# Attention stage of a four-layer kernel: one unit per row with all four heads, and a rewritten order of work

## The chip, the cores and the metric

The kernel runs on one core of one Trainium2 chip. The metric is the device time of one execution in microseconds (us), lower is better. The engines are named as in the profile: PE is TensorE (PEld its weight loads), DVE is VectorE, ACT is ScalarE, POOL is GpSimd, SP is SyncE, which here only issues DMAs. PEclk is the share of the TensorE clock that the chip granted.

## The reference, cut to what matters

A 256 x 256 grid of positions with 128 channels goes through four layers. Each layer adds its result to its input. The change concerns the first one, an attention with four heads of 32 channels along every row of the grid:

```python
z = layernorm(groupnorm(x))                      # 256 x 256 x 128
q, k, v = heads(z @ Wq), heads(z @ Wk), heads(z @ Wv)   # 4 heads of 32
g = sigmoid(heads(z @ Wg)); bias = z @ Wb        # bias: 256 x 256 x 4
scores = einsum('bijhd,bikhd->bijkh', q, k) / sqrt(32) + bias[:, None]
a = softmax(scores, axis=-2)                     # over k, within one row i
o = einsum('bijkh,bikhd->bijhd', a, v)
x = x + (g * o).reshape(b, n, n, 128) @ Wout
```

So every row i of 256 positions is its own attention problem: four 256 x 256 score matrices, one for each head.

## The kernel before

The stages follow one another: statistics of x, `row_norm` (layer norm and the bias projection, written to memory as `zs` and `bs`), `attention`, then layers 1 to 3. All data are 32-bit floats. A matmul of such data is recorded as two MATMULs (two passes), each with its weight load; a transpose is one.

`attention` holds channels on the partitions and positions along the free axis. It works in 32 blocks (NB) of 2048 positions, that is 8 rows. For a block, `load_block` issues two DMAs of 1 MB on SP (z and x), and `project` makes q, k, v and g in sixteen pieces of 512 positions, each through the PSUM tile `mm`; q and g are taken out by ACT (L287, L289), k and v by DVE (L285, L281).

A unit u is one row and a pair of heads (hp), so a block has 16 units (UB) and the stage 512. For one unit:

- `scores`: for two tiles of queries (jt) and two heads (h), q times k with 32 channels on the partitions (L297). Each head sits on its own 32 partitions, so the two heads use two row tiles of the PE array and write into two PSUM banks. Then DVE adds the bias and takes the row's minimum of the negative in four instructions (L308), which also write the result to `e`.
- `exps`: four exponentials on ACT with their sums (L323), a reciprocal on DVE (L331), the scaling of `e` on POOL (L332).
- `transposes`: eight 128 x 128 transposes into `tp0` and `tp1` (L341), taken out by ACT (L344) and DVE (L346) as `at0` and `at1`.
- `product`: v times the transposed weights (L355), 32 output columns for each head, so the two heads use two column tiles of the array, accumulated over kt into `op`.

`gate` (L369, DVE) multiplies a finished row of `op` by the gate. `out` (L382 to L386), for every second row, multiplies by Wout into `mm`, adds x on DVE, takes the statistics on DVE, and with each block's last one stores x1.

`manual_schedule()` keeps every engine's instructions in the order in which the code issues them. The loop over u issues: the gate of a row finished in the turn before, scores of u + 2, exponentials of u + 1, transposes of u, projections of the next block (in turns 5 to 15 of a block, two of them in turns 5 to 9), product of u - 1, and `out` where it is due. [...] two buffers of two banks for the scores, `tp0`, `tp1`, `op`, `mm`.

The four-tile helper `four` in `row_norm` (L167) matters as well: it issues four matmuls of 512 columns with 32 output columns each, into four 32-partition strips of one bank.

Of the kernel before, what the change touches and what calls it, by code (L numbers as in the profile page):

```python
# [10 lines left out]
F32 = mybir.dt.float32  # L11
AF = mybir.ActivationFunctionType
ALU = mybir.AluOpType
# [4 lines left out]
P = 128  # L18
S = 256
# [216 lines left out]
def attention(c, x, x1, zs, bs, w, stats):  # L236
# [3 lines left out]
    tc, nc = c.tc, c.nc  # L240
    BL, NH = 2048, 4
    NB = NPOS // BL
    UB = 16
    N = UB * NB
    with ExitStack() as a:
        one = a.enter_context(tc.tile_pool(name="l0b_one", bufs=1))
        io = a.enter_context(tc.tile_pool(name="l0b_io", bufs=2))
        wk = a.enter_context(tc.tile_pool(name="l0b_wk", bufs=2))
        ps2 = a.enter_context(tc.tile_pool(name="l0b_p2", bufs=2, space=PSUM))
        ps1 = a.enter_context(tc.tile_pool(name="l0b_p1", bufs=1, space=PSUM))  # L250
        bias = one.tile([P, NH, 2, S], F32, name="l0b_bias")

        wo = one.tile([P, P], F32, name="l0b_wo")
        nc.vector.tensor_scalar(wo, w["o"], 0.5, None, ALU.mult)
        for jt in range(2):
            nc.sync.dma_start(
                bias[:, :, jt, :], bs[:, bass.ts(jt, P), :].rearrange("h p k -> p h k")
            )
        blocks, es, tops, dens, ats, ops, gates = ({} for _ in range(7))

        def load_block(b):
            k = blocks[b] = {}
            for n, src in (("z", zs), ("x", x)):
                k[n] = io.tile([P, BL], F32, name=f"l0b_{n}")
                nc.sync.dma_start(k[n], src[:, bass.ts(b, BL)])
            for n in "qkg":
                k[n] = wk.tile([P, BL], F32, name=f"l0b_{n}")
            k["v"] = wk.tile([P, 16, P], F32, name="l0b_v")

        def project(b, i):  # L270
            k = blocks[b]
            j, n = i // 4, "kqvg"[i % 4]
            cs = bass.ts(j, CH)
            bank = ("mm", "tp0", "tp1")[i % 3] if b == 0 else "mm"
            mm = ps1.tile([P, CH], F32, name=f"l0b_{bank}")
            if n == "v":
                for m in range(4):
                    nc.tensor.matmul(
                        mm[:, bass.ts(m, P)], k["z"][:, bass.ts(4 * j + m, P)], w["v"], start=True, stop=True
                    )  # L280
                nc.vector.tensor_copy(k["v"][:, 4 * j : 4 * j + 4].rearrange("p m o -> p (m o)"), mm)  # L281
                return
            nc.tensor.matmul(mm, w[n], k["z"][:, cs], start=True, stop=True)
            if n == "k":
                nc.vector.tensor_copy(k["k"][:, cs], mm)  # L285
            elif n == "q":
                nc.scalar.activation(k["q"][:, cs], mm, AF.Copy, scale=float(1.0 / np.sqrt(32)))  # L287
            else:
                nc.scalar.activation(k["g"][:, cs], mm, AF.Tanh, scale=0.5)  # L289

        def scores(u):
            k, r, hp = blocks[u // UB], u % UB // 2, u % 2
            sc = ps2.tile([P, 2, 2, S], F32, name="l0b_sc")
            for jt in range(2):
                for h in range(2):
                    hs = slice(32 * (2 * hp + h), 32 * (2 * hp + h) + 32)
                    nc.tensor.matmul(  # L297
                        sc[:, h, jt],
                        k["q"][hs, bass.ds(r * S + jt * P, P)],
                        k["k"][hs, bass.ts(r, S)],  # L300
                        start=True,
                        stop=True,
                    )

            e = es[u] = wk.tile([P, 4, S], F32, name="l0b_e", bufs=4)
            top = tops[u] = wk.tile([P, 4], F32, name="l0b_top")
            for i in range(4):
                nc.vector.tensor_tensor_reduce(  # L308
                    e[:, i],
                    sc[:, i // 2, i % 2],  # L310
                    bias[:, 2 * hp + i // 2, i % 2],
                    -1.0,
                    3.0e38,
                    ALU.add,
                    ALU.min,
                    accum_out=top[:, i : i + 1],
                )

        def exps(u):
            e, top = es[u], tops.pop(u)  # L320
            den = wk.tile([P, 4], F32, name="l0b_den")
            for i in range(4):
                nc.scalar.activation(  # L323
                    e[:, i],
                    e[:, i],
                    AF.Exp,
                    scale=-1.0,
                    bias=top[:, i : i + 1],
                    accum_out=den[:, i : i + 1],
                )  # L330
            nc.vector.reciprocal(den, den)  # L331
            nc.gpsimd.tensor_tensor(e, e, den[:, :, None].to_broadcast([P, 4, S]), ALU.mult)  # L332

        def transposes(u):
            e = es.pop(u)
            for kt in range(2):
                tp = ps1.tile([P, CH], F32, name=f"l0b_tp{kt}")
                tp = tp.rearrange("p (h j q) -> p h j q", h=2, j=2)
                for h in range(2):
                    for jt in range(2):  # L340
                        nc.tensor.transpose(tp[:, h, jt], e[:, 2 * h + jt, bass.ts(kt, P)], c.ident)  # L341
                at = ats[u, kt] = wk.tile([P, 2, S], F32, name=f"l0b_at{kt}")
                if kt == 0:
                    nc.scalar.copy(at, tp.rearrange("p h j q -> p h (j q)"))  # L344
                else:
                    nc.vector.tensor_copy(at, tp.rearrange("p h j q -> p h (j q)"))  # L346

        def product(u):
            k, r, hp = blocks[u // UB], u % UB // 2, u % 2
            if hp == 0:  # L350
                ops[u // 2] = ps1.tile([P, S], F32, name="l0b_op")
            for kt in range(2):
                for h in range(2):
                    hs = slice(32 * (2 * hp + h), 32 * (2 * hp + h) + 32)
                    nc.tensor.matmul(  # L355
                        ops[u // 2][hs],
                        k["v"][:, 2 * r + kt, hs],
                        ats[u, kt][:, h],
                        start=kt == 0,
                        stop=kt == 1,  # L360
                    )
            for kt in range(2):
                del ats[u, kt]

        def gate(row):
            b, r = divmod(row, 8)
            if r % 2 == 0:
                gates[row // 2] = wk.tile([P, CH], F32, name="l0b_gated")
            nc.vector.scalar_tensor_tensor(  # L369
                gates[row // 2][:, bass.ts(r % 2, S)],  # L370
                blocks[b]["g"][:, bass.ts(r, S)],
                1.0,
                ops.pop(row),
                ALU.add,
                ALU.mult,
            )

        def out(pair):
            b, j = divmod(pair, 4)
            xt, cs = blocks[b]["x"], bass.ts(j, CH)  # L380
            mm = ps1.tile([P, CH], F32, name="l0b_mm")
            nc.tensor.matmul(mm, wo, gates.pop(pair), start=True, stop=True)  # L382
            nc.vector.tensor_tensor(xt[:, cs], mm, xt[:, cs], ALU.add)
            nc.vector.bn_stats(stats[:, pair, :], xt[:, cs])
            if j == 3:
                nc.sync.dma_start(x1[:, bass.ts(b, BL)], xt)  # L386
                del blocks[b]

        a.enter_context(tc.manual_schedule())
        load_block(0)  # L390
        for i in range(UB):
            project(0, i)
        scores(0)
        scores(1)
        exps(0)
        for u in range(N + 3):
            b, i = divmod(u, UB)
            if u >= 3 and u % 2 == 1:
                gate((u - 3) // 2)
            if i == 4 and b + 1 < NB:  # L400
                load_block(b + 1)
            if u + 2 < N:
                scores(u + 2)
            if u + 1 < N:
                exps(u + 1)
            if u < N:
                transposes(u)
            if 5 <= i and b + 1 < NB:
                project(b + 1, i - 5)
            if 1 <= u <= N:  # L410
                product(u - 1)
            if u >= 5 and (u - 5) % 4 == 0:
                out((u - 5) // 4)
            if 5 <= i < 10 and b + 1 < NB:
                project(b + 1, i + 6)

# [1492 lines left out]
```

## Time and profile before

| | us |
|---|---|
| median of 3 runs (29926.62 to 29932.67) | 29930.62 |
| the profiled execution, its own time | 29939.38 |
| its span, first to last instruction | 29937.2 |
| attention, first to last product (L355 at 583.0 and 2882.8) | 2299.8 |
| one block in the steady part (x1 stores at 1527.79 and 1600.27) | 72.48 |
| the same for one row | 9.06 |
| layer 1, of the same span (first matmul 2910, last 26302) | some 23390 |

Attention is 7.8% of the whole; one per cent of it is 23 us. In a timeline, the first number of a line is the start in us from the span's start, the second the length, then engine, source line, operation, out<-in, the shape and how many instructions were merged; the bracket tells how long the engine had been idle, and who ended that. In a table of windows, each engine has its busy us and its number of instructions, and then follow PEclk, DMA share and GB/s. In a table of groups, the numbers are busy us, mean ns of one instruction, and the idle time before it with its releasers.

### The profile page before, as it was taken

To read this page: it belongs to the slowest core of one execution; us is meant where nothing else is said; L and a number is where in the kernel's file an instruction comes from. 1 tells how busy PE (TensorE), PEld (TensorE's weight loads), DVE (VectorE), ACT (ScalarE), POOL (GpSimd) and SP (SyncE) were. 2 spreads that over 40 slices of the span, in tenths; PEclk is the share of its full clock that TensorE was granted. 3 is DMA by queue.
4 is the path that set the end of the run, shared out by engine and by line. 5 is a ranking of instruction groups with operands and counts; after the bars stand their busy time and mean duration, and the time that the engine had idled before them with its cause. 6 is when DMAs were issued, how large, how long until landed. Compare 5 with 4: busy or idle time off the path is not lost.

```text
span 29937.2 us, 548536 instructions
## 1 busy us (share of the span) xinstructions
PE 27671.1 (92%) x213108; PEld 19370.2 (65%) x213108; DVE 27302.1 (91%) x30333; ACT 20859.9 (70%) x40976; POOL 23130.3 (77%) x6484
## 2 busy tenths in 40 slices
PE   7999989999999999999999999999999999989877
PEld 2555467777777777777777777777777776344443
DVE  6666999999999999999999999999999999833899
ACT  3666877777777777777777777777777776422677
POOL 2444789999999999999999999999999998300000
PEclk9999999999999999999999999999999999999999
DMA  4111455555555666666666666666666666773111
GB/s 158 43 43 54 183 190 190 188 189 187 190 190 191 194 194 194 193 194 194 201 206 206 206 206 206 206 205 208 207 206 207 208 208 210 225 224 107 41 34 34
DMA packets 2930533, 5178.80 MB, mean 173 GB/s; under 512 B 705127, under 2 KB 1969528, under 8 KB 2876342
## 3 DMA queue, kind: packets, MB, share of 16 engines
q1 hardware_dynamic: 2791954, 5072.44, 52.0%
q10 hardware_dynamic: 135972, 71.27, 0.8%
q8 instruction: 1677, 27.48, 0.4%
q14 instruction: 930, 7.62, 0.1%
HBM read 4433.10 MB, written 709.89 MB: 172 GB/s over the span
## 4 chain that ended last, share of the span: by engine, by line
PE 58%; ACT 21%; DVE 8%; issue 2%; DMA 1%; SPq 0%; POOL 0%; DVEq 0%; ACTq 0%; POOLq 0%
PE l1b_y L686 20%; PE l1b_pair L843 16%; ACT l1b_da L865 7%; PE l1b_mi L796 4%; PE l1b_mi L701 3%; PE l1b_mi L771 3%; PE l1b_mi L686 3%; ACT l1b_tail L791 2%; DVE l1b_h L884 2%; ACT l1b_tail L783 2%; ACT l1b_tail L790 2%; ACT l1b_mi L784 2%; PE l2f_fp L1495 2%; PE l2f_op L1502 1%; DVE l1a_mm L522 1%
## 5 line engine op out<-in xcount | busy, mean ns | idle before, releaser
L898 POOL TENSOR_TENSOR l1b_hc<-l1b_h,l1b_cc 128x2048 f32<-128x2048 f32 x4096 | 18612.2, 4558 | 240.5 <-PE l1b_mi L796 64.4
L884 DVE TENSOR_TENSOR_SCAN l1b_h<-l1b_da,l1b_state,l1b_pair 128x512 f32<-128x512 f32 x12288 | 14584.5, 1257 | 33.6 <-PE l1b_pair L843 32.8
L686 PE MATMUL l1b_y<-ident,l1b_hc 128*128 128x128 f32 x65536 | 8645.4, 277 | 4.2 <-POOL l1b_hc L898 4.2
L686 PEld LDWEIGHTS l1b_y<-ident,l1b_hc 128*128 128x128 f32 x65536 | 7143.2, 141 | 2225.3 <-issue 1646.7
L865 ACT ACTIVATE l1b_da<-l1b_dl,l_alog 128x512 f32<-128x512 f32 x12288 | 8169.7, 714 | 0.0
L843 PE MATMUL l1b_pair<-l1b_diag,l1b_dut 64*128 64x128 f32 x98304 | 7267.8, 285 | 144.2 <-DVE l1b_h L884 142.4
L843 PEld LDWEIGHTS l1b_pair<-l1b_diag,l1b_dut 64*128 64x128 f32 x98304 | 6056.1, 184 | 1145.6 <-issue 642.3
L884 DVE TENSOR_TENSOR_SCAN l1b_h<-l1b_pair,l1b_state,l1b_db 128x512 f32<-128x512 f32 x4096 | 5004.4, 1264 | 3.2 <-ACT l1b_pair L865 3.2
L865 ACT ACTIVATE l1b_pair<-l1b_dl,l_alog 128x512 f32<-128x512 f32 x4096 | 2831.5, 691 | 66.5
L823 POOL TENSOR_TENSOR l1b_db<-l1b_bb,l1b_dus 128x1024 f32<-128x1024 f32 x1024 | 2431.8, 2375 | 176.8 <-ACT l1b_dus L817 103.2
L332 POOL TENSOR_TENSOR l0b_e<-l0b_e,l0b_den 128x1024 f32<-128x1024 f32 x512 | 969.0, 1893 | 1372.8 <-DVE l0b_den L331 726.4
L892 ACT COPY l1b_state<-l1b_h 128x4 f32<-128x4 f32 x4096 | 800.0, 195 | 1745.7 <-DVE l1b_h L884 1745.4
L783 ACT ACTIVATE l1b_tail<-l1b_mi 128x512 f32<-128x512 f32 x1024 | 615.1, 601 | 1886.5 <-PE l1b_mi L771 1886.5
L796 PE MATMUL l1b_mi<-l1b_tail,ident 128*128 128x512 f32 x2048 | 1153.4, 645 | 442.9 <-ACT l1b_tail L791 442.9
L940 ACT COPY l1b_yt<-l1b_y 128x512 f32<-128x512 f32 x1024 | 599.8, 586 | 1107.5 <-PE l1b_y L686 1107.5
L686 PE MATMUL l1b_mi<-ident,l1b_dus 128*128 128x128 f32 x4096 | 765.5, 309 | 609.1 <-ACT l1b_dus L817 604.0
L823 DVE TENSOR_TENSOR l1b_db<-l1b_bb,l1b_mi 128x1024 f32<-128x1024 f32 x1024 | 1250.8, 1221 | 37.7 <-DMA l1b_bb<-l1b_bc 2.5
L308 DVE CUSTOM_DVE_ANT_0 l0b_e<-l0b_sc,l0b_bias 128x256 f32<-128x256 f32 x2048 | 745.5, 420 | 414.4 <-PE l0b_sc L297 411.0
L686 PEld LDWEIGHTS l1b_mi<-ident,l1b_dus 128*128 128x128 f32 x4096 | 570.8, 209 | 821.7 <-ACT l1b_dus L817 785.9
L771 PE MATMUL l1b_mi<-l1b_xd,l_dtw 41*128 41x512 f32 x2048 | 1044.1, 589 | 0.3 <-ACT l1b_bt L733 0.3
L701 PE MATMUL l1b_mi<-l1b_xc,l_xproj 128*40 128x512 f32 x2048 | 981.6, 602 | 42.6 <-DMA l1b_xc<-l_xc 42.3
L323 ACT ACTIVATE l0b_e<-l0b_e,l0b_top 128x256 f32<-128x256 f32 x2048 | 1012.2, 498 | 0.9 <-DVE l0b_top L308 0.9
(288 smaller groups left out, 32766.6 us busy)
## 6 DMA issues: line engine op xcount, KB each, us to landing
l1b_cc<-l1b_bc SPq DMA_DIRECT2D x4096, 512.0 KB
l1b_diag<-l1b_far SPq DMA_DIRECT2D x1024, 768.0 KB
l1b_bb<-l1b_bc SPq DMA_DIRECT2D x1024, 512.0 KB
l1b_xc<-l_xc SPq DMA_DIRECT2D x128, 1024.0 KB
l_y<-l1b_yo SPq DMA_DIRECT2D x128, 1024.0 KB
l1b_xc<-l_xct SPq DMA_DIRECT2D x256, 512.0 KB
l_y<-l1b_yo SPq DMA_DIRECT2D x256, 512.0 KB
l_xc<-l1a_o SPq DMA_DIRECT2D x64, 1024.0 KB
```

The costliest lines, as they stand in the source:

```text
L323: nc.scalar.activation(e[:, i], e[:, i], AF.Exp, scale=-1.0, bias=top[:, i : i + 1], accum_out=den[:, i : i + 1],)
L332: nc.gpsimd.tensor_tensor(e, e, den[:, :, None].to_broadcast([P, 4, S]), ALU.mult)
L686: nc.tensor.matmul(to, part, c.ident[0 : part.shape[0], 0 : part.shape[0]], start=start, stop=True, is_transpose=True, skip_group_check=True,)
L701: nc.tensor.matmul(mi[:40], w["xproj"][:, dh, k, :], in_block(blocks[ch][0], ch, dh), start=dh == 0, stop=dh == 1,)
L771: nc.tensor.matmul(mi, w["dt"][:, chunks[ch][0], dh * P : dh * P + P], xds[ch % 3][0:41], start=True, stop=True,)
L783: nc.scalar.activation(soft[u], mi, AF.Abs)
L796: nc.tensor.matmul(mi, c.ident, soft.pop(u), start=False, stop=True, skip_group_check=True)
L823: eng.tensor_tensor(dbs[i], bbs[i], du[:, None, :].to_broadcast([P, 2, CH]), ALU.mult)
L843: nc.tensor.matmul(to[:, b, rows], duts[u % 2][rows, b], diag[on_pe[i] // 3][rows, b, :, n : n + 2], start=True, stop=True, skip_group_che ...
L865: nc.scalar.activation(to[:, j], dls[u], AF.Exp, scale=w["A"][:, k, dh, n : n + 1])
L884: nc.vector.tensor_tensor_scan(h_, a_, d_, states[k][:, dh, at : at + 1], ALU.mult, ALU.add)
L898: nc.gpsimd.tensor_tensor(hc, hs[g], ccs[g % NQ], ALU.mult)
```

## The change

The unit becomes a row with all four heads: 8 units a block, 256 in all. `scores` issues its eight matmuls over four row tiles into one PSUM tile of four banks that has one buffer, where there were two buffers of two banks. `product` issues its eight matmuls over four column tiles. The other helpers are split into smaller ones (`biased` and `exps` by head, `norm`, `transposes` and `turned` by pair of heads), and the loop over rows issues them in another order. The gate of row r - 1 now follows its product in the same turn, and `out` follows that gate where r is even. Two projections are made in each turn, an even one (k or v, taken out by DVE) and an odd one (q or g, by ACT), in place of sixteen in eleven of sixteen turns. Blocks are loaded two ahead, and z and x have three buffers. The number of matmuls, transposes, exponentials, copies and DMAs stays as it was.

```diff
-    UB = 16
+    UB = 8
-        io = a.enter_context(tc.tile_pool(name="l0b_io", bufs=2))
+        io = a.enter_context(tc.tile_pool(name="l0b_io", bufs=3))
-        ps2 = a.enter_context(tc.tile_pool(name="l0b_p2", bufs=2, space=PSUM))
...
-        def scores(u):
-            k, r, hp = blocks[u // UB], u % UB // 2, u % 2
-            sc = ps2.tile([P, 2, 2, S], F32, name="l0b_sc")
+        def scores(r):
+            if r >= N:
+                return
+            k, i = blocks[r // UB], r % UB
+            sc = scs[r] = ps1.tile([P, NH, 2, S], F32, name="l0b_sc")
             for jt in range(2):
-                for h in range(2):
-                    hs = slice(32 * (2 * hp + h), 32 * (2 * hp + h) + 32)
+                for h in range(NH):
+                    hs = slice(32 * h, 32 * h + 32)
                     nc.tensor.matmul(
...
+        def biased(r, h):
...
+            for jt in range(2):
                 nc.vector.tensor_tensor_reduce(
...
+        def exps(r, h):
...
+        def norm(r, hp):
...
+        def transposes(r, hp):
...
+        def turned(r, hp):
             for kt in range(2):
+                at = ats[r, hp, kt] = wk.tile([P, 2, S], F32, name=f"l0b_at{hp}{kt}")
+                copy = nc.vector.tensor_copy if kt else nc.scalar.copy
+                copy(at.rearrange("p h q -> p (h q)"), tps[kt])
+
+        def product(r):
...
+            op = ops[r] = ps1.tile([P, S], F32, name="l0b_op")
+            for kt in range(2):
+                for h in range(NH):
+                    hs = slice(32 * h, 32 * h + 32)
                     nc.tensor.matmul(
-                        ops[u // 2][hs],
+                        op[hs],
...
         load_block(0)
-        for i in range(UB):
+        load_block(1)
+        for i in range(16):
             project(0, i)
...
+        for r in range(N + 2):
+            b, i = divmod(r, UB)
+            if i == 3 and b + 2 < NB:
+                load_block(b + 2)
+            biased(r + 1, 0)
+            exps(r + 1, 0)
+            if r < N:
+                transposes(r, 0)
+            biased(r + 1, 1)
+            exps(r + 1, 1)
+            if r < N:
+                turned(r, 0)
+            if b + 1 < NB:
+                project(b + 1, 2 * i)
+            norm(r + 1, 0)
+            if r < N:
+                transposes(r, 1)
+            biased(r + 1, 2)
+            exps(r + 1, 2)
+            biased(r + 1, 3)
+            exps(r + 1, 3)
+            if r < N:
+                turned(r, 1)
+            scores(r + 2)
+            if b + 1 < NB:
+                project(b + 1, 2 * i + 1)
+            norm(r + 1, 1)
+            if 1 <= r <= N:
+                product(r - 1)
+                gate(r - 1)
+            if r >= 2 and r % 2 == 0:
+                out(r // 2 - 1)
```

More of the change, by code (lines that the diff above doesn't have):

```diff
@@ L258, in attention @@
             )
-        blocks, es, tops, dens, ats, ops, gates = ({} for _ in range(7))
+        blocks, scs, es, tops, dens, tps, ats, ops, gates = ({} for _ in range(9))
         def load_block(b):
@@ L289, in project @@
                 nc.scalar.activation(k["g"][:, cs], mm, AF.Tanh, scale=0.5)
-        def scores(u):
-            k, r, hp = blocks[u // UB], u % UB // 2, u % 2
-            sc = ps2.tile([P, 2, 2, S], F32, name="l0b_sc")
+        def scores(r):
[3 more added lines that the diff above has]
+            sc = scs[r] = ps1.tile([P, NH, 2, S], F32, name="l0b_sc")
             for jt in range(2):
-                for h in range(2):
-                    hs = slice(32 * (2 * hp + h), 32 * (2 * hp + h) + 32)
+                for h in range(NH):
+                    hs = slice(32 * h, 32 * h + 32)
                     nc.tensor.matmul(
                         sc[:, h, jt],
-                        k["q"][hs, bass.ds(r * S + jt * P, P)],
-                        k["k"][hs, bass.ts(r, S)],
+                        k["q"][hs, bass.ds(i * S + jt * P, P)],
+                        k["k"][hs, bass.ts(i, S)],
                         start=True,
@@ L303, in scores @@
                     )
-            e = es[u] = wk.tile([P, 4, S], F32, name="l0b_e", bufs=4)
-            top = tops[u] = wk.tile([P, 4], F32, name="l0b_top")
-            for i in range(4):
+        def biased(r, h):
+            if r >= N:
+                return
+            if h == 0:
+                es[r] = wk.tile([P, NH, 2, S], F32, name="l0b_e", bufs=3)
+                tops[r] = wk.tile([P, NH, 2], F32, name="l0b_top")
+                dens[r] = wk.tile([P, NH, 2], F32, name="l0b_den")
+            for jt in range(2):
                 nc.vector.tensor_tensor_reduce(
-                    e[:, i],
-                    sc[:, i // 2, i % 2],
-                    bias[:, 2 * hp + i // 2, i % 2],
+                    es[r][:, h, jt],
+                    scs[r][:, h, jt],
+                    bias[:, h, jt],
                     -1.0,
@@ L315, in scores @@
                     ALU.min,
-                    accum_out=top[:, i : i + 1],
+                    accum_out=tops[r][:, h, jt : jt + 1],
                 )
[L319 to L322, printed above, removed]
+        def exps(r, h):
+            if r >= N:
+                return
+            e, top, den = es[r], tops[r], dens[r]
+            for jt in range(2):
                 nc.scalar.activation(
-                    e[:, i],
-                    e[:, i],
+                    e[:, h, jt],
+                    e[:, h, jt],
                     AF.Exp,
                     scale=-1.0,
-                    bias=top[:, i : i + 1],
-                    accum_out=den[:, i : i + 1],
-                )
+                    bias=top[:, h, jt : jt + 1],
+                    accum_out=den[:, h, jt : jt + 1],
+                )
+        def norm(r, hp):
+            if r >= N:
+                return
+            hs = slice(2 * hp, 2 * hp + 2)
+            e, den = es[r][:, hs], dens[r][:, hs]
             nc.vector.reciprocal(den, den)
-            nc.gpsimd.tensor_tensor(e, e, den[:, :, None].to_broadcast([P, 4, S]), ALU.mult)
-        def transposes(u):
-            e = es.pop(u)
+            nc.gpsimd.tensor_tensor(e, e, den[:, :, :, None].to_broadcast([P, 2, 2, S]), ALU.mult)
+        def transposes(r, hp):
+            e = es[r]
             for kt in range(2):
-                tp = ps1.tile([P, CH], F32, name=f"l0b_tp{kt}")
+                tp = tps[kt] = ps1.tile([P, CH], F32, name=f"l0b_tp{kt}")
                 tp = tp.rearrange("p (h j q) -> p h j q", h=2, j=2)
@@ L340, in transposes @@
                     for jt in range(2):
[L341 to L351, printed above, removed]
-            for kt in range(2):
-                for h in range(2):
-                    hs = slice(32 * (2 * hp + h), 32 * (2 * hp + h) + 32)
+                        nc.tensor.transpose(
+                            tp[:, h, jt], e[:, 2 * hp + h, jt, bass.ts(kt, P)], c.ident
+                        )
+        def turned(r, hp):
+            for kt in range(2):
+                at = ats[r, hp, kt] = wk.tile([P, 2, S], F32, name=f"l0b_at{hp}{kt}")
+                copy = nc.vector.tensor_copy if kt else nc.scalar.copy
+                copy(at.rearrange("p h q -> p (h q)"), tps[kt])
+        def product(r):
+            k, i = blocks[r // UB], r % UB
+            op = ops[r] = ps1.tile([P, S], F32, name="l0b_op")
+            for kt in range(2):
+                for h in range(NH):
+                    hs = slice(32 * h, 32 * h + 32)
                     nc.tensor.matmul(
-                        ops[u // 2][hs],
-                        k["v"][:, 2 * r + kt, hs],
-                        ats[u, kt][:, h],
+                        op[hs],
+                        k["v"][:, 2 * i + kt, hs],
+                        ats[r, h // 2, kt][:, h % 2],
                         start=kt == 0,
@@ L361, in product @@
                     )
-            for kt in range(2):
-                del ats[u, kt]
+            for hp in range(2):
+                for kt in range(2):
+                    del ats[r, hp, kt]
         def gate(row):
@@ L390, in attention @@
         load_block(0)
-        for i in range(UB):
+        load_block(1)
+        for i in range(16):
             project(0, i)
         scores(0)
-        scores(1)
[L395 to L415, printed above, removed]
+        for h in range(NH):
+            biased(0, h)
+            exps(0, h)
+        norm(0, 0)
+        norm(0, 1)
+        scores(1)
+        for r in range(N + 2):
[30 more added lines that the diff above has]
+                out(r // 2 - 1)
 def conv_block(c, x1, ab, xc, xct):
```

## The prediction

> **What bounds it now.** I cut the attention stage out by the windows view and set `row_norm`, the stage before it, beside it.
>
> ```profile
> core 0: us, PE busy (x) PEld busy (x) DVE busy (x) ACT busy (x) POOL busy (x), PEclk, DMA share, GB/s
> 300.00:400.00 100.00, 81.94 (x239) 25.53 (x236) 62.74 (x40) 26.43 (x31) 19.11 (x16) 0.90 0.46 166
> 553.00:2885.00 2332.00, 2205.64 (x14336) 1251.18 (x14336) 1538.35 (x5887) 1443.45 (x4866) 968.97 (x512) 1.00 0.12 43
> ```
>
> In attention PE is busy 95% of the time, DVE 66%, ACT 62%, POOL 42%, DMA 12%, and PE has the whole clock. `row_norm` has PE idle less than a fifth of the time, yet PEclk is 0.90 there. Next, PE's timeline in attention; starts matter, since matmuls overlap:
>
> ```profile
> 1522.14 1.13 PE L297 MATMUL l0b_sc<-l0b_k,l0b_q 32*128 32x256 f32 x8
> 1523.89 1.09 PE L341 MATMUL l0b_tp<-ident,l0b_e 128*128 128x128 f32 x8 [0.62 <-POOL l0b_e L332]
> 1524.91 1.06 PE L355 MATMUL l0b_op<-l0b_at,l0b_v 128*32 128x256 f32 x8
> 1525.90 1.12 PE L382 MATMUL l0b_mm<-l0b_gated,l0b_wo 128*128 128x512 f32 x2
> 1526.96 1.13 PE L297 MATMUL l0b_sc<-l0b_k,l0b_q 32*128 32x256 f32 x8
> ```
>
> Start to start, `product` takes 0.99, `out` 1.06, transposes 1.02, scores 1.06 (1526.96 to the next transposes at 1528.02), a projection 0.95 to 0.99 (1504.12 to 1505.08). A block of 16 units is 16 x (1.06 + 1.02 + 0.99) + 16 x 0.96 + 4 x 1.06 = 68.7 us, and idling 3.8 more, to the 72.48 us between two stores of x1. So **PE's queue is the bound**, and its longest idle gap in the waits view is 0.9 us. By groups:
>
> ```profile
> L323 ACT ACTIVATE l0b_e<-l0b_e,l0b_top 128x256 f32<-128x256 f32 x1853 | 915.8, 498 | 0.0
> L332 POOL TENSOR_TENSOR l0b_e<-l0b_e,l0b_den 128x1024 f32<-128x1024 f32 x464 | 878.2, 1893 | 1224.3 <-DVE l0b_den L331 620.4 <-PE l0b_mm L283 535.5 <-PE l0b_tp L341 68.4
> L308 DVE CUSTOM_DVE_ANT_0 l0b_e<-l0b_sc,l0b_bias 128x256 f32<-128x256 f32 x1852 | 674.3, 420 | 375.1 <-PE l0b_sc L297 372.0
> ```
>
> DVE's timeline gives the pitches: L308 0.345 (1503.31, 1503.66, 1504.00), the copy of tp 0.58, of k or v 0.60, add 0.72, statistics 0.61, reciprocal 0.09. ACT's: exponential 0.49, copy 0.48. Now `row_norm`'s PE:
>
> ```profile
> 306.31 2.73 PE L145 MATMUL l0a_dp<-l0a_x,l_scaled 128*128 128x512 f32 x4 [2.26 <-ACT l0a_sq L161]
> 308.97 1.94 PE L167 MATMUL l0a_var<-l0a_sq,avg 128*32 128x512 f32 x8
> 310.84 1.98 PE L186 MATMUL l0a_bc<-l0a_rs,l_pick 128*128 128x512 f32 x4
> 312.75 1.06 PE L167 MATMUL l0a_bp<-l0a_d,l_wb 128*32 128x512 f32 x8
> ```
>
> Two things are to be seen. Eight MATMULs on four column tiles take 1.06 us, as two on the whole array do: four column tiles run at once. And the same eight take 1.94 us shortly after a gap of 2.26 us: **half clock**. The gap returns every 13.4 us (next at 319.7); a half-clock stretch of about 3 us in each gives PEclk 0.89, which is what the window shows.
>
> [...] four row tiles it does not show, only two (eight passes of 256 in 1.06 us). [...]
>
> **Part by part.**
>
> *Tiles.* Scores of a row are 16 passes, four at a time: 4 x 0.216 + 0.2 of switching = 1.06, for 2.12 before. Bounds: 1.06 (no tile is quicker than its own four passes) and 1.93 (only two at a time); I take 1.06. Product: 0.99 for 1.98. PE's queue needs 2.05 us less a row, 6.6 in place of 8.6.
>
> *Order.* This decides. DVE's queue now is, in a turn: gate(r-1), [add, statistics], four L308, copy of tp, copy of k or v, reciprocal, four L308, copy of tp, reciprocal. The scores have one buffer, so scores(r+2) waits for the last L308 of r+1, and the first L308 of r+2 is queued behind gate(r-1), which waits for product(r-1), which stands on PE behind scores(r+2) and a projection. With two buffers and the gate a turn later, that loop was open. It is closed now; from one gate (time 0) to the next:
>
> - gate 0.345; four L308 to 1.73; copy to 2.30; k or v to 2.90. The reciprocal needs four exponentials: they start at 0.83 (0.345 + 0.43 for the first L308 with its accumulator, 0.06 to ACT), the last begins at 2.30 and is seen by DVE at 2.99 (0.59 with its own accumulator, 0.10 to DVE). Reciprocal to 3.08, four L308 to 4.46, finished and seen by PE at 4.60.
> - PE: scores to 5.66, projection to 6.72 (1.06 after a switch of tiling, as for `out`), product to gate 1.10 (1505.08 to 1506.18 before). **7.82 us** for a row without `out`.
> - With `out`: its matmul waits for the gate (0.47), the add starts 1.17 later (1525.90 to 1527.07 before), then 0.72 and 0.61: the first L308 begins at 2.97, not 0.345. **10.45 us**.
>
> A pair of rows takes 18.27, a block 73.1 us against 72.48; 128 pairs make **+19 us**. PE's second transposes nearly tie with this path: they wait for ACT's copy, queued behind those four exponentials (2.79 + 0.58 + 0.06), to 3.43 and end by 4.5. What is freed on PE turns into idle time: between the even projection (0.95 for the first transposes and 0.86 after them: to about 1.8 in a row without `out`, 3.3 behind one) and these transposes (3.43, or 6.06 with `out`), gaps of 1.6 and **2.75 us**.
>
> *Clock.* The longer gap exceeds the one that halves the clock in `row_norm`. What follows it on PE, transposes, scores, projection, product, is on the path. A window of 3.4 us at half clock defers half of what PE would stream, about 85% of it: 1.45 us. Bounds: 0, and both gaps of every pair, 256 x 1.45 = 371; full clock is the cap, so no gain. I take one at each long gap and at a fifth of the short ones (estimates): 154 x 1.45 = **+223 us**.
>
> *At nothing.* POOL's two scalings of 1.89 a row are released at about 3.2 and 5.9 of a turn and needed at 7.8 and 11.2; if POOL were 2.5 us later, PE would wait. ACT has 5.4 of 9.1 us; its q or g copy waits behind nothing on the path. Loads on SP stand two blocks (146 us) ahead, behind the store of an x that lies two turns back; without that lead a 1 MB load is still 40 us early. Projections: same number, one DVE copy in each row, counted above. First rows and last block: a few us either way.
>
> Sum on the profiled execution: 29939.4 + 19 + 223 = 30181; the median of the runs lies 8.8 lower: **30173**.
>
> **Rivals.**
> - *PE's saving arrives.* For it: PE 95% busy, and 2.05 us a row is freed. Against: the closed loop. If gate and `out` did not hold DVE, its 5.7 us (8 x 0.345 + 2 x 0.58 + 0.60 + 0.345 + 0.18 + half of 1.33) and PE's 6.6 leave some 7.5 a row with waits: (7.5 - 9.06) x 256 = -400, 29530. It decides if a row without `out` falls under about 6.8 us. Chance 0.12.
> - *Loop closed, clock full.* [...] the gap of 0.9 before never cost clock. 29950. Chance 0.14.
> - *Four row tiles run two by two*, so the change does not do what it says: +0.87 on the path of every row, +223 more: 30395. Chance 0.06.
> - The forecast: loop and half clock, chance 0.68.
>
> **Numbers.** 0.2% is 60 us, about what a measurement of this kernel can tell from no change. Slower by more: the forecast, the pairs, and a little of the full-clock case: 0.76. Within: 0.12. Faster: 0.12. The range from 29940 to 30300 holds the forecast with its clock bounds and the full-clock case; it leaves out 0.18.
>
> **What would show it.** PEclk in attention between 0.80 and 0.92; PE waiting on ACT's l0b_at before l0b_tp for some 2 us a row; DVE's l0b_gated waiting on PE's l0b_op for about 2 us a row; ACT waiting on l0b_top; 16 score MATMULs in 1.06 us where the clock is full; `out` in every other turn with PE waiting for the gate. A block below 70 us proves the loop wrong; PEclk 1.00 proves the clock step wrong; scores at 1.9 us under full clock prove the tiles wrong.

## The result and the profile after

| | before | after |
|---|---|---|
| median of the runs shown with the result, us | 29931.64 | 30243.05 |
| lowest to highest, us | 29926.62 to 29936.53 | 30237.12 to 30243.54 |
| the profiled execution, us | 29939.38 | 30243.02 |
| one block of attention at full clock, us | 72.5 | 73.9 |

The changed kernel takes 311 us more: ratio 1.0104, interval [1.0086, 1.0121]. The forecast was 30173, 70 us too low. The sign was right, and so were the two parts of the mechanism, the closed loop and the half clock; the count of half-clock stretches was not.

The whole difference lies in attention. The windows view of the kernel after, over that stage (columns as in the windows views of the prediction):

```profile
553.00:3187.00 2634.00, 1981.78 (x14336) 1137.93 (x14336) 1554.99 (x5886) 1456.72 (x4865) 969.16 (x512) 0.89 0.10 38
```

The same 14336 MATMULs now stand in 2634 us instead of 2332. DVE, ACT and POOL have, within about 1%, the busy time that they had (1538, 1443 and 969 us). PE's fell from 2206 to 1982, and that although part of it ran at half clock: PEclk is 0.89 where it was 1.00. So PE was relieved, the other engines were not, and the stage grew longer around them.

PE's timeline of the kernel after, two rows at full clock and the start of a half-clock stretch:

```profile
1504.48 1.10 PE L399 MATMUL l0b_mm<-l0b_gated,l0b_wo 128*128 128x512 f32 x2 [0.64 <-DVE l0b_gated L386]
...
1510.14 1.06 PE L355 MATMUL l0b_tp<-ident,l0b_e 128*128 128x128 f32 x8 [2.63 <-ACT l0b_at L363]
1511.23 1.15 PE L298 MATMUL l0b_sc<-l0b_k,l0b_q 32*128 32x256 f32 x16
1512.30 1.12 PE L282 MATMUL l0b_mm<-l0b_z,l_wg 128*128 128x512 f32 x2
1513.36 1.07 PE L371 MATMUL l0b_op<-l0b_at,l0b_v 128*32 128x256 f32 x16
1514.36 1.09 PE L355 MATMUL l0b_tp<-ident,l0b_e 128*128 128x128 f32 x8
...
1518.04 1.06 PE L355 MATMUL l0b_tp<-ident,l0b_e 128*128 128x128 f32 x8 [1.73 <-ACT l0b_at L363]
...
1522.96 1.10 PE L399 MATMUL l0b_mm<-l0b_gated,l0b_wo 128*128 128x512 f32 x2 [0.64 <-DVE l0b_gated L386]
...
1528.63 1.37 PE L355 MATMUL l0b_tp<-ident,l0b_e 128*128 128x128 f32 x8 [2.63 <-ACT l0b_at L363]
1529.93 2.09 PE L298 MATMUL l0b_sc<-l0b_k,l0b_q 32*128 32x256 f32 x16
1531.95 1.46 PE L282 MATMUL l0b_mm<-l0b_z,l_wg 128*128 128x512 f32 x2
1533.35 1.07 PE L371 MATMUL l0b_op<-l0b_at,l0b_v 128*32 128x256 f32 x16
```

Four things are to be seen. The sixteen score MATMULs take 1.07 us from start to start (1511.23 to 1512.30) and the product's sixteen 1.00 (1513.36 to 1514.36), so four tiles do run at once. A pair of rows, `out` to `out`, takes 18.48 us. PE has two long idle gaps in it, 2.63 and 1.73 us. And after the next long gap the same scores take 2.02 us (1529.93 to 1531.95): from the transposes to the product it is 4.72 us instead of 3.22, so this half-clock stretch cost 1.50.

The waits view of the kernel after, 700 to 3050 us, for PE and DVE (us in total, times, longest):

```profile
PE l0b_tp L355 <- ACT l0b_at L363: 500.1, 229, 2.6
```
```profile
DVE l0b_gated L386 <- PE l0b_op L371: 677.0, 229, 4.5
```

Each engine waits for another one in every row: 500.1 us in 229 rows is 2.2 a row on PE, 677.0 is 3.0 on DVE, and ACT's 733.1 in the next view, over all 256 rows, is 2.9. That is what a closed loop looks like: no engine is full. The groups view, at the two places that the prediction showed of the kernel before:

```profile
L331 ACT ACTIVATE l0b_e<-l0b_e,l0b_top 128x256 f32<-128x256 f32 x2048 | 1015.4, 497 | 733.1 <-DVE l0b_top L315 733.1
L315 DVE CUSTOM_DVE_ANT_0 l0b_e<-l0b_sc,l0b_bias 128x256 f32<-128x256 f32 x2048 | 737.9, 417 | 1.8 <-PE l0b_sc L298 1.3 <-issue 0.5
```

One exponential takes 497 ns, as it did (498), but ACT now stands idle 733 us ahead of them, where there was nothing. The addition of the bias hardly waits any more (1.8 us; 414 before, over as many instructions): it is held by the gate ahead of it on DVE.

### The profile page after: what moved, and what is told of

Read it like the earlier page. It is cut to its first block, busy times and chain, and to the rows that moved or that the text cites. A ratio compares the mean times of both kernels' runs of the same rounds, so it can differ in the third digit from the quotient of the medians.

```text
span 30240.9 us, 547097 instructions
## 1 busy us (share of the span) xinstructions
PE 27448.1 (91%) x213108; PEld 19262.9 (64%) x213108; DVE 27313.4 (90%) x30333; ACT 20874.4 (69%) x40976; POOL 23133.2 (76%) x6484
## 3 DMA queue, kind: packets, MB, share of 16 engines
q1 hardware_dynamic: 2791954, 5072.44, 51.7%
## 4 chain that ended last, share of the span: by engine, by line
PE 63%; ACT 23%; DVE 10%; issue 2%; DMA 1%; SPq 0%; POOL 0%; ACTq 0%; DVEq 0%; POOLq 0%
PE l1b_y L719 20%; PE l1b_pair L876 16%; ACT l1b_da L898 7%; PE l1b_mi L829 4%; PE l1b_mi L734 3%; PE l1b_mi L804 3%; PE l1b_mi L719 3%; ACT l1b_tail L824 2%; ACT l1b_tail L816 2%; DVE l1b_h L917 2%; ACT l1b_tail L823 2%; ACT l0b_e L331 2%; ACT l1b_mi L817 2%; PE l2f_fp L1528 2%; PE l2f_op L1535 1%
## 5 line engine op out<-in xcount | busy, mean ns | idle before, releaser
L331 ACT ACTIVATE l0b_e<-l0b_e,l0b_top 128x256 f32<-128x256 f32 x2048 | 1015.4, 497 | 733.1 <-DVE l0b_top L315 733.1
L355 PE MATMUL l0b_tp<-ident,l0b_e 128*128 128x128 f32 x4096 | 598.4, 294 | 561.5 <-ACT l0b_at L363 560.2
```

What stands on the lines that cost most here:

```text
L331: nc.scalar.activation(e[:, h, jt], e[:, h, jt], AF.Exp, scale=-1.0, bias=top[:, h, jt : jt + 1], accum_out=den[:, h, jt : jt + 1],)
```

## The experiments

**Fill PE's idle time, nothing else.** Three matmuls of 256 columns, whose result nobody reads, go into PE's gap ahead of the second transposes. They take 1.46 us at full clock, less than either gap, and stand where PE waited anyway. They are work that the computation doesn't need.

```diff
+        def idle(n):
+            d = ps1.tile([P, S], F32, name="l0b_op")
+            for _ in range(n):
+                nc.tensor.matmul(d, c.ident, bias[:, 0, 0], start=True, stop=True)
...
+            if 1 <= r < N:
+                idle(3)
             norm(r + 1, 0)
```

> The changed kernel with three more matmuls of 256 columns a row (two passes each, some 1.4 us), whose result nobody reads, put on PE into the gap before the second transposes. They add work and take away no wait. Theory (closed loop, and the clock halved by PE's gaps): the gap of 1.7 us still holds them, so the path is as long as before, the clock stays at 1.00 in attention, a block takes 73.9 us, and the time is some 29980 us, 265 below the changed kernel. Rival (the clock is a by-product and costs nothing, the loop itself is longer than was worked out): 30243 or up to 300 us more.

Measured: 29989.24, ratio to the kernel before 1.0017 [1.0010, 1.0024]. More work on PE, and 254 us less than the changed kernel. The windows view, 1000 to 2000 us, of this run:

```profile
1000.00:2000.00 1000.00, 867.11 (x6703) 542.47 (x6702) 658.52 (x2486) 614.09 (x2052) 408.89 (x216) 1.00 0.12 45
```

PEclk is 1.00. So the loss splits in two: **the clock is worth 254 us, the loop at full clock 53** (29989.24 against 29936.53, the median of the kernel before at that time). The loop did not move: the stores of x1 stand 73.9 us apart (1324.92 and 1398.86), which is the block at full clock of the changed kernel.

**One matmul in place of three.** The same with `idle(1)`.

> The same with one more matmul a row in place of three. Theory: [...] about half of the half-clock windows are left (some 90 in place of 172): about 30110 us, PEclk in attention 0.94. Rival (no effect of the clock): 30243 or somewhat more.

Measured: 30146.5, ratio 1.0070 [1.0053, 1.0086]. PEclk between 1000 and 2000 us is 0.93 here, 0.89 in the changed kernel. The clock records of the changed kernel hold 1.00 and 0.50 alone; so half-clock time is twice what is missing to 1, 14% against 22% of the time, and 14/22 of 254 is 162 above the full-clock run: 30151. The cost goes with the half-clock time, not with the matmuls added.

**Open the loop: the gate a turn later.** The gate of row r - 2 follows the exponentials of head 1, and `out` moves behind the scores of odd turns. All instructions stay.

```diff
             exps(r + 1, 1)
+            if r >= 2:
+                gate(r - 2)
...
             scores(r + 2)
+            if r >= 3 and r % 2 == 1:
+                out((r - 3) // 2)
...
                 product(r - 1)
-                gate(r - 1)
-            if r >= 2 and r % 2 == 0:
-                out(r // 2 - 1)
```

> The changed kernel with the gate of a row issued one turn later, after the first four bias instructions on DVE, and the output of two rows issued after the scores of the odd turns. Nothing else. Theory (the loop runs through the gate and the output in DVE's queue): a block drops from 81.9 to about 66.4 us, with hardly a half-clock window left; 29740 us, faster than both kernels. Rival (PE's work or ACT's exponentials set the row, the gate only waits along): 30243, no change to speak of. Rival (four row tiles slow the scores): little change either.

Measured: 29729.51, ratio 0.9931 [0.9916, 0.9946]: 514 us below the changed kernel, 207 below the one before. The stores of x1 stand 66.2 us apart (1518.01 and 1584.23). The waits of DVE and of PE, 1000 to 2000 us:

```profile
DVE l0b_gated L386 <- PE l0b_op L371: 35.4, 60, 0.6
```
```profile
PE l0b_sc L298 <- DVE l0b_top L315: 102.6, 121, 0.9
```

DVE's wait for the product fell to 35.4 us (289 in the same stretch of the changed kernel); what is late next is the scores, for their single buffer, 0.85 us a row. PE's longest wait is 0.9 us now, and PEclk is 1.00 without any filling. So 254 of the 514 us are the clock, and 260 are the loop (29989.24 to 29729.51, both at full clock). Where the gate and `out` stand decided the sign of this change. The gate was not moved alone; the next run moves `out` alone.

**Only `out` later.** The gate stays where the change put it; `out` moves to the odd turns, ahead of the product.

```diff
+            if r >= 3 and r % 2 == 1:
+                out((r - 3) // 2)
             if 1 <= r <= N:
                 product(r - 1)
                 gate(r - 1)
-            if r >= 2 and r % 2 == 0:
-                out(r // 2 - 1)
```

> The changed kernel with only the output of two rows moved one turn later, ahead of the product, the gate left where it is. Theory: the loop is still closed through the gate but loses the matmul of the output and DVE's wait for it in every second row: 71.3 us a block at full clock, about 76.8 with the half-clock windows that stay; 30080 us. Rival (the gate alone is the wait, the output costs nothing): 30243.

Measured: 30033.85, ratio 1.0032 [1.0019, 1.0046], 46 us under what I expected, PEclk 0.94 between 1000 and 2000 us. So `out` on the path is part of the loop's cost, 209 us with the clock that came back, but the loop is still closed without it: DVE waits 139.9 us for the product, in every second row (289 in the changed kernel). A pair between two `out` at full clock takes 17.89 us (1528.16 to 1546.05, PEclk 1.00), less than the 18.12 of before; the half clock that is left is what makes this run slower than the kernel before.

**Move what PE waits for.** The first copies go ahead of the exponential of head 1.

```diff
-            exps(r + 1, 1)
             if r < N:
                 turned(r, 0)
+            exps(r + 1, 1)
```

> The changed kernel with one edit: ACT's and DVE's copies of the first transposes go ahead of the exponential of head 1. The largest wait on PE is for ACT's copy, 500 us in the stage; rival theory (that wait is the cost, so an earlier copy brings some of it back): faster than the changed kernel, up to 250 us, near 30000. My theory (that wait is slack of PE's, and the path runs through DVE and the exponentials, which the earlier copy delays by 0.48 us a row): a block of 77 us at full clock, about 83.6 with the half clock, near 30285, 30 to 60 slower than the changed kernel.

Measured: 30337.38, ratio 1.0134 [1.0119, 1.0149]: 94 slower than the changed kernel; I had 30 to 60. PE's wait for that copy did shrink, between 1000 and 2000 us from 211.4 to 113.6, and the kernel got slower: the wait was slack. PE's timeline of this run holds something more:

```profile
1495.83 1.10 PE L399 MATMUL l0b_mm<-l0b_gated,l0b_wo 128*128 128x512 f32 x2 [0.64 <-DVE l0b_gated L386]
...
1500.52 1.06 PE L355 MATMUL l0b_tp<-ident,l0b_e 128*128 128x128 f32 x8 [1.65 <-ACT l0b_at L363]
1503.06 1.15 PE L298 MATMUL l0b_sc<-l0b_k,l0b_q 32*128 32x256 f32 x16 [1.48 <-DVE l0b_top L315]
...
1515.29 1.10 PE L399 MATMUL l0b_mm<-l0b_gated,l0b_wo 128*128 128x512 f32 x2 [0.64 <-DVE l0b_gated L386]
```

A pair takes 19.46 us at full clock, 0.98 more than in the changed kernel. The wait was split in two gaps of 1.65 and 1.48, the longest of PE's waits is 1.8 (700 to 2100 us), and still PEclk between 1000 and 2000 us is 0.92.

**The same instructions in an order that opens the loop everywhere.**

```diff
             biased(r + 1, 0)
-            exps(r + 1, 0)
             if r < N:
                 transposes(r, 0)
             biased(r + 1, 1)
-            exps(r + 1, 1)
+            biased(r + 1, 2)
+            if r >= 2:
+                gate(r - 2)
             if r < N:
                 turned(r, 0)
             if b + 1 < NB:
                 project(b + 1, 2 * i)
+            exps(r + 1, 0)
+            if 1 <= r <= N:
+                product(r - 1)
+            exps(r + 1, 1)
+            biased(r + 1, 3)
             norm(r + 1, 0)
             if r < N:
                 transposes(r, 1)
-            biased(r + 1, 2)
             exps(r + 1, 2)
-            biased(r + 1, 3)
             exps(r + 1, 3)
             if r < N:
                 turned(r, 1)
+            if r >= 3 and r % 2 == 1:
+                out((r - 3) // 2)
             scores(r + 2)
...
-            if 1 <= r <= N:
-                product(r - 1)
-                gate(r - 1)
-            if r >= 2 and r % 2 == 0:
-                out(r // 2 - 1)
```

> The same instructions as the changed kernel, in an order that opens the loop: the gate of row r-2 ahead of the copies of row r, product(r-1) between the exponentials of heads 0 and 1, the third addition of the bias ahead of the gate, out two turns later and ahead of scores(r+2). Theory (the loop through gate, exponentials, reciprocal and scores costs the change its saving; PE's work itself is 2 us a row smaller): PE becomes the bound again, a block takes 51.5 us of work on PE and somewhat more with its waits (up to 57), the clock is full, attention takes 1690 to 1800 us: 29280 to 29400. Rival (the saving on PE was small, and the stage can't go below what it was with the gate a turn later, 66.4 us a block): about 29730. Rival (DVE is now the next bound at about 62 us a block with its waits): about 29600.

Measured: 29284.59, ratio 0.9784 [0.9767, 0.9800]. **648 us faster than the kernel before**, 958 faster than the changed one, with the same instructions. The windows view over its whole stage, and one row of PE's timeline:

```profile
553.00:2240.00 1687.00, 1659.92 (x14336) 1017.67 (x14336) 1505.20 (x5889) 1407.65 (x4865) 963.95 (x512) 0.99 0.16 60
```
```profile
1505.93 1.15 PE L298 MATMUL l0b_sc<-l0b_k,l0b_q 32*128 32x256 f32 x16
1507.01 1.13 PE L282 MATMUL l0b_mm<-l0b_z,l_wg 128*128 128x512 f32 x2
1507.97 1.04 PE L355 MATMUL l0b_tp<-ident,l0b_e 128*128 128x128 f32 x8
1508.84 1.10 PE L282 MATMUL l0b_mm<-l0b_z,l_wk 128*128 128x512 f32 x2
1509.96 1.07 PE L371 MATMUL l0b_op<-l0b_at,l0b_v 128*32 128x256 f32 x16
1510.97 1.09 PE L355 MATMUL l0b_tp<-ident,l0b_e 128*128 128x128 f32 x8
1511.99 1.15 PE L298 MATMUL l0b_sc<-l0b_k,l0b_q 32*128 32x256 f32 x16
```

There is no bracket in it: PE waits for nothing, a row without `out` takes 6.06 us, the stores of x1 stand 51.7 apart, and PE is busy 98% of the stage. By the sums of the prediction, 525 of the 648 are the change's relief of PE, 2.05 us a row, and 122 are the 3.8 us of waits that a block had before.

**Two tiles at a time, by the order of issue.** In the order just shown, and in the changed kernel's own, the loops inside `scores` and `product` run through heads 0 and 1 for both halves before heads 2 and 3.

```diff
-            for jt in range(2):
-                for h in range(NH):
+            for jt, h in [(jt, 2 * hp + h) for hp in range(2) for jt in range(2) for h in range(2)]:
```

> The order of the run before, but the scores and the product issue two tiles at a time (heads 0 and 1 for both halves of the row, then heads 2 and 3)[...]. Theory (PE is the bound in this order and four tiles at once save 0.9 to 1.0 us each in scores and product): 331 us slower than the run before, a block about 61.9 us, near 29610. Rival (four tiles bring nothing over two, or PE isn't the bound of that order): within 60 us of the run before.

> The changed kernel in its own order, with the scores and the product issuing two tiles at a time. Scores and product lie on the path in this order. Theory (four row tiles and four column tiles do run together in the changed kernel, two and two in this one): 0.87 us a row more in the scores, some of it taken back where PE's idle windows are filled and the clock stays up; near 30460, 217 over the changed kernel. Rival (the scores and the product aren't on the path, or two tiles are as quick as four): within 60 us of the changed kernel, 30243.

Measured: 29284.70, against 29284.59 with the tiles in turn; and 30243.22, against 30243.05. Both rivals' numbers, yet neither rival is shown: the edit did not do what I meant it to. The groups of the first of these two, within 60 ns (1506.30 to 1506.36 us):

```profile
L297 PE MATMUL l0b_sc<-l0b_k,l0b_q 32*128 32x256 f32 x4 | 0.5, 478 | 0.0
```

Four passes begin within these 60 ns, and the four that begin from 1506.635 us on are followed by four from 1506.851 on, 0.216 us later; all sixteen take 1.08 (1506.32 to 1507.40), as with the tiles in turn. So four are at work together in this order too. Why the edit did not bring about two at a time was not shown: the records name neither the head nor the place in the queue.

**Two tiles at a time, by a change of tiling between them.** In the open order, the pairs of heads stand on either side of other work.

```diff
             if 1 <= r <= N:
-                product(r - 1)
+                product(r - 1, 0)
...
                 transposes(r, 1)
+            if 1 <= r <= N:
+                product(r - 1, 1)
...
-            scores(r + 2)
+            scores(r + 2, 0)
             if b + 1 < NB:
                 project(b + 1, 2 * i + 1)
+            scores(r + 2, 1)
```

> The order with the open loop (the fifth run), but the scores of heads 0 and 1 and of heads 2 and 3 stand on either side of the odd projection, and the product of heads 0 and 1 and of heads 2 and 3 on either side of the second transposes. PE changes its tiling between them, so that no more than two tiles can be at work together, which issuing the tiles in another order did not bring about. Theory (PE is the bound in that order, and four tiles at once save it 1.06 us of scores and 0.99 of product a row): 525 us slower than that order, a block near 68.1 us, 29810, clock full. Rival (a saving on PE that the other engines' work would hide anyway): DVE's and ACT's work allows about 47 to 62 us a block, so less than 330 more, under 29620.

Measured: 30031.36, ratio 1.0032 [1.0019, 1.0044]: 747 slower than the open order, not 525. The rival (a saving that other engines would hide) falls. From PE's timeline, a row without `out`:

```profile
1501.21 1.06 PE L375 MATMUL l0b_op<-l0b_at,l0b_v 128*32 128x256 f32 x8 [0.80 <-DVE l0b_gated L389]
...
1504.21 1.13 PE L300 MATMUL l0b_sc<-l0b_k,l0b_q 32*128 32x256 f32 x8
1505.27 1.12 PE L282 MATMUL l0b_mm<-l0b_z,l_wq 128*128 128x512 f32 x2
1506.33 1.13 PE L300 MATMUL l0b_sc<-l0b_k,l0b_q 32*128 32x256 f32 x8
1507.39 1.09 PE L357 MATMUL l0b_tp<-ident,l0b_e 128*128 128x128 f32 x8
```

Each half of the scores takes as long as the whole on four tiles, 1.06. But my split made a wait as well, 0.80 here and 0.78 on the mean (82.0 us in 105 rows): the second half of the scores ends at 1507.4, six additions and the gate follow on DVE (6 x 0.345 + 0.34 = 2.4), and the product needs that gate to free its bank. Of the 747, 0.78 x 256 = 200 is this wait. The remaining 547 is 2.1 us a row, and the tiles' share of it was put at 2.05. The split adds changes of tiling too, which the prediction put at 0.2 us each (an estimate: 1.06 us for eight passes on two tiles, less 4 x 0.216), so this run measures a group of four tiles against two groups of two, and not the tiles without their changes.

## Why the prediction came out as it did

- *PE is the bound before.* Confirmed by the open order: less work on PE and its waits taken away gave 648 us, the sum of the two. PE's work for a row, put at 6.6 (8.59 less 2.05 is 6.54), is 6.46 there: 51.7 us a block, with next to no waits.
- *Tiles: 1.06 for scores, 0.99 for the product.* 1.07 and 1.00. The rival "two by two" (30395) is out: its 1.9 us at full clock appears nowhere. In this trace, sixteen passes of 256 columns on four row tiles take what eight on two tiles took (1.07 us, and 1.06 before).
- *The closed loop.* Its path is the one in the trace. DVE's timeline of the kernel after:

```profile
1503.91 0.42 DVE L386 SCALAR_TENSOR_TENSOR l0b_gated<-l0b_g,l0b_op 128x256 f32<-128x256 f32 x1 [2.04 <-PE l0b_op L371]
...
1506.95 0.41 DVE L315 CUSTOM_DVE_ANT_0 l0b_e<-l0b_sc,l0b_bias 128x256 f32<-128x256 f32 x1
...
1509.63 0.18 DVE L345 RECIPROCAL l0b_den<-l0b_den 128x4 f32<-128x4 f32 x1
...
1514.50 0.42 DVE L386 SCALAR_TENSOR_TENSOR l0b_gated<-l0b_g,l0b_op 128x256 f32<-128x256 f32 x1 [2.04 <-PE l0b_op L371]
```

  Gate to first addition 3.04 (predicted 2.97), from there to the reciprocal 2.68 (2.65), from the first addition to the next gate 7.55 (7.48), gate to gate with `out` 10.59 (10.45). The terms that were short: from the gate to `out` it is 0.57 (1503.91 to 1504.48), taken as 0.47, and from the product to the gate 1.14 (1513.36 to 1514.50), taken as 1.10; the rest is hundredths. A pair is 18.48, not 18.27. Against the 18.12 of before that is 0.36 x 128 = **46 us, where the sum had 19**; the filled run, which shows the loop without the clock, gives 53.
- *The gaps.* 2.63 and 1.73, predicted 2.75 and 1.6.
- *The clock.* The price of one half-clock stretch was right: 1.45 predicted, 1.50 in the timeline above. So was its length, put at 3.4 us: in the trace of before, behind the 2.26 us gap of `row_norm`, PEclk is 0.50 from 307.42 to 310.83 us, 3.41. **The count was the step that failed**, "one at each long gap and at a fifth of the short ones", 154, and with it the rule behind it, that the length of a gap decides: the 2.26 us gap of `row_norm` was read as long enough.

  The clock records in the trace, which the windows view reads as PEclk, have half clock in windows of 3.41 us. Between 700 and 3050 us there are 153 of them for 115 pairs of rows, which makes 170 for all 128. Filling the gaps gave back 254 us, 1.49 for each of them, where the sum had 223.

  The records repeat a pattern every three pairs of rows: of three long gaps one is followed by one half-clock window, one by two and one by none, and of three short gaps one is followed by one. So it was one for each long gap on the average, but the rule "one at each" did not hold, and that its number came out was luck; a third of the short gaps were followed by one, not a fifth. What decides between them was not shown. Of the stretches below, the first holds a long gap whole, and the half-clock stretch of the timeline above follows it at 1529.25. The other two share a long gap between them (1568.96 to 1571.59), and the clock stays full:

```profile
1525.84:1529.25 3.41, 0.78 (x8) 0.65 (x7) 3.37 (x18) 3.13 (x12) 0.81 (x1) 1.00 0.00 0
1566.80:1570.21 3.41, 2.16 (x17) 1.76 (x15) 3.12 (x11) 1.31 (x5) 0.00 (x0) 1.00 0.50 199
1570.21:1573.63 3.42, 2.03 (x24) 1.58 (x24) 3.06 (x12) 3.25 (x14) 1.89 (x1) 1.00 0.99 331
```

  PEclk is 0.50 from 1529.25 to 1532.67, and 1.00 from 1573.63 to 1577.04.
- *At nothing.* The stage's POOL, loads and projections stayed out of it: PE's transposes wait for POOL for 1.1 us in all, and outside attention PE's busy time differs by 1 us of some 25470. DVE's and ACT's work is no smaller: 1555 and 1457 us, for 1538 and 1443.
- *Rivals.* "PE's saving arrives" needed the loop open; it is what the later gate (29730) and the open order (29285) show. "Clock full" is what the filled run shows, 29989, where I put it at 29950.

Together 46 to 53 and 254 make 300 to 307 of the 311 measured; what is left is within the spread of the runs: the medians of the kernel before alone, in the groups of runs used here, lie 6 us apart (29931.64 to 29937.34).

## What to carry to other kernels

Work taken from the engine that is the bound is worth nothing if the same edit closes a loop through the others: follow one buffer around (who frees it, what stands ahead of the freeing instruction in its queue, what that waits for) and compare the loop's length with the engine's work. An instruction that waits for the newest result, as the gate did, belongs a turn later in a queue that keeps the order of the code, as `manual_schedule()` makes it here; that, with `out` moved as well, was worth 514 us, the clock included, and its full version 958. Where an engine other than PE sets the pace, look at PEclk too: behind a gap of 2.63 us on PE the scores took 2.02 us here, and 1.07 at full clock.

## What the runs showed of the hardware

- PEclk by PE's gaps, between 1000 and 2000 us: 0.89 with gaps of 2.63 and 1.73 us (the changed kernel), 0.92 with gaps of at most 1.8 us, two close together (copies first), and 1.00 with at most 1.3 (filled), at most 0.9 (the later gate) and none (the open order). One gap's length does not tell: the same 2.63 us was followed by one half-clock window of 3.41 us, by two or by none, and these runs do not show what decides it.
- Idle time on PE was cheaper filled: 1.46 us a row of useless matmuls made this kernel 254 us faster.
- The order in which the tiles of one group of matmuls are issued made no difference (0.1 and 0.2 us in 29285 and 30243), as far as eight passes of one pair of tiles ahead of the other's.
